# Layer 2's column sums: running sums on GpSimd in place of 25 products with ones each

## The chip, the core and the metric

The kernel runs on one core of a Trainium2 chip. The metric is the device time of one execution in microseconds (us). Before the change it is 3435.26 us, the median of six runs between 3418.8 and 3440.62.

Short names for the engines: PE is TensorE, the matrix engine, whose weight loads are listed as PEld; DVE is VectorE, ACT is ScalarE, POOL is GpSimd, SP is SyncE, which here only issues DMAs. PE writes its products to PSUM, which POOL doesn't read in this kernel.

## The reference

A graph network of four layers on 3125 nodes with 256 features and 100000 edges: a graph convolution, an attention layer, a gated layer and a convolution with a decoder. After each the result is added to `x` and normalized along the features. The change lies in the last step of the attention layer and the first step of the gated one (layer 2), cut here to what matters:

```python
x = _layernorm(x + attention(x, ...), axis=-1)      # layer 1
# layer 2
mean = jnp.mean(feat, axis=0)                       # over the 3125 nodes, for each feature
var = jnp.var(feat, axis=0)
h = (feat - mean) * jax.lax.rsqrt(var + EPS) * gamma + beta
feat_in, feat_out = h @ W_in + b_in, h @ W_out + b_out
a_in = segment_sum(feat_in[src] * iw[:, None], dst)
a_out = segment_sum(feat_out[dst] * ow[:, None], src)
...
```

So layer 2 needs two sums over all nodes for each of the 256 features: of `x`, and of the squares of `x` less its mean.

## The kernel before

The nodes are laid out in 25 blocks (`NBK`) of 128 rows: `x[:, b, :]` is block b, 128 partitions by 256 float32. Block 0 holds few nodes (`FEW_ROWS`, 53), the others are full. A layer's sum over edges is done as a product with a dense slab: for block b, `weighted_slab` builds 25 tiles of 128 x 128 edge weights, and `apply_f32` multiplies them with the features of all 25 blocks, adding up in the PSUM tile `acc` (L783, 25 products of 128 x 257 for a block).

A slab is built in two halves of 13 and 12 tiles. For each half DVE makes the one-hot tiles `os` and `od` (L729) by comparing keys with a row of column numbers, and three products `wo` of `od` with the three bfloat16 parts of the weights (L909); both inputs of all of these lie in SBUF. PE multiplies `wo` with `os` into PSUM tiles `slab` of four tiles each (L755, three buffers), and ACT copies these to SBUF as `slab_f` (L756). `wo` has four buffers, so DVE can't run far ahead of PE. The weights of the next block are split by four short DVE instructions (L899 to L903).

**Attention** is a loop over the 25 blocks, in the pool `layer1`: build the slab, multiply with `H`, then `den` and its reciprocal on DVE (L972, L973), Relu on ACT (`tmp`, L975), add to `x` on DVE (L976), and `norm(b)`: statistics on DVE (L696 to L698), a square root on ACT (L702), reciprocal and the scaling of `x[:, b, :]` on DVE (L703, L704). From L704 on, block b of `x` is final for layer 2's sums. In block 0 `bounds()` takes some extremes for a flag.

**Layer 2's first pass**, in the pools `layer2` and `layer2a`, is again a loop over the 25 blocks: `aggregate` builds the slab and multiplies it with `x`, ACT copies the result (`sums`, L1090), SP writes it to `a_in`, and then `stage(b)` does a share of the side work:

- stage 0 forms the sum of `x` over the nodes: 25 products with a 128 x 128 matrix of ones (`ones_f`; for block 0 `few`, which has ones only in the rows that hold nodes), all into one PSUM tile `mm` (L1027). DVE scales it to `mean` (L1028).
- each stage takes two blocks: POOL subtracts `mean` (L1033, into `away`, two buffers), ACT squares it in place (L1034). The next stage multiplies each of the two with ones into the PSUM tile `var` (named `look` in the profile, L1030).
- stages 14 and 15 copy the keys into another order on POOL (`keys_t`, `keyd_t`, L1038). Stage 16 loads weights and multiplies them together (L1050, PSUM tile `mm`; the pool of `mm` has a single buffer). Stages 17 to 19 make `scl`, `cr`, `cols` and biases from `var`.

The second pass uses the turned keys and these factors, and ends each block with gates and a normalization; layer 3 follows.

The order of the work in attention and layer 2 isn't written out by hand: a planner walks through the program with costs of its own and gives each engine, whenever it is free, the earliest instruction of the program that is ready by those costs. The result is a fixed order for each engine and queue. On the chip each engine then keeps that order and waits by semaphores. So an instruction can run long before its place in the program (keys_t's copy of stage 14 runs ahead of stage 0's subtract), and one that is late on the chip holds up whatever the planner put behind it on its engine. `tc.keep_in_program_order(o)` ties an instruction behind the one before it in the program on the same engine.

Of the kernel before, what the change touches and what calls it, by code (L numbers as in the profile page):

```python
# [8 lines left out]
F32 = mybir.dt.float32  # L9
# [3 lines left out]
OP = mybir.AluOpType  # L13
# [5 lines left out]
P = 128  # L19
# [18 lines left out]
NBK = 25  # L38
# [14 lines left out]
KD = ND // P  # L53
# [46 lines left out]
def dense_path(ctx: ExitStack, tc: tile.TileContext, a: dict, out: bass.AP, flag: bass.AP):  # L100
    nc = tc.nc
    N, D = 3125, ND
# [19 lines left out]
    ones_f = top.tile([P, P], F32, name="ones_f")  # L122
# [517 lines left out]
    psM = ctx.enter_context(tc.tile_pool(name="d_psM", bufs=1, space=PSUM))  # L640
# [15 lines left out]
    x = x1[:, :, 1:D + 1]  # L656
# [268 lines left out]

    with tc.tile_pool(name="layer1", bufs=2) as pool:
        den = pool.tile([P, NBK], F32, name="den", bufs=1)

        def largest(v, n=1):

            vt = psT.tile([P, P], F32, name="tp")
            nc.tensor.transpose(vt[:n, :], v, ident)
            r = pool.tile([n, 1], F32, name=f"largest{n}", bufs=6)
            nc.vector.tensor_reduce(r, vt[:n, :], axis=AX.X, op=OP.max)
            return r


        bmax = pool.tile([P, NBK], F32, name="bmax", bufs=1)
        q_by_target = q.rearrange("p (d t) -> p d t", d=NBK)
        nc.vector.tensor_reduce(bmax, q_by_target, axis=AX.X, op=OP.max)  # L940
        r = largest(bmax, NBK)
        c = psT.tile([P, NBK], F32, name="tp")
        nc.tensor.matmul(c, r.to_broadcast([NBK, P]), ident[:NBK, :NBK], start=True, stop=True)
        nc.vector.tensor_tensor(q_by_target, q_by_target, c[:, :, None].to_broadcast([P, NBK, TS]), op=OP.subtract)
        nc.scalar.activation(q, q, AF.Exp)


        nc.vector.tensor_reduce(ends[:, 2:3], s1, axis=AX.X, op=OP.max)
        nc.vector.tensor_reduce(ends[:, 3:4], s1, axis=AX.X, op=OP.min)
        e4 = pool.tile([P, 4], F32, name="e4", bufs=1)  # L950

        def bounds():
            for i in range(4):
                nc.vector.tensor_scalar(e4[:, i:i + 1], ends[:, i:i + 1], 1.0 if i % 2 == 0 else -1.0, None, op0=OP.mult)
            m4 = [largest(e4[:, i:i + 1]) for i in range(4)]
            zs = []
            for i, sg in ((0, 1.0), (1, -1.0)):
                z = pool.tile([1, 1], F32, name=f"z{i}", bufs=1)
                nc.vector.tensor_tensor(z, m4[i], m4[i + 2], op=OP.add)
                nc.vector.tensor_scalar(z, z, sg, None, op0=OP.mult)  # L960
                nc.vector.scalar_tensor_tensor(z, z, 0.01, z, op0=OP.mult, op1=OP.max)
                zs.append(z)
            nc.vector.tensor_sub(zs[0], zs[0], zs[1])
            nc.vector.tensor_scalar(flag[:, 1:2], zs[0], SPREAD, None, op0=OP.is_ge)

        for b in range(NBK):
            w3 = wk.tile([P, 3, TS, 2], BF, name="w3")
            weights_split(w3, wk, q[:, b * TS:(b + 1) * TS], TS, 2)
            slab = weighted_slab(pool, b, keys, keyd, w3)
            p = apply_f32(slab, H, D + 1)  # L970

            nc.vector.tensor_scalar(den[:, b:b + 1], p[:, D:], 1e-37, None, op0=OP.max)  # L972
            nc.vector.reciprocal(den[:, b:b + 1], den[:, b:b + 1])  # L973
            y = wk.tile([P, D], F32, name="tmp")
            nc.scalar.activation(y, p[:, :D], AF.Relu, scale=den[:, b:b + 1])  # L975
            nc.vector.tensor_add(x[:, b, :], x[:, b, :], y)  # L976
            norm(b)
            if b == 0:
                bounds()

# [6 lines left out]
    with tc.tile_pool(name="layer2", bufs=1) as pool:  # L989
# [27 lines left out]

        with tc.tile_pool(name="layer2a", bufs=1) as pa:
            mean, var = pa.tile([P, D], F32, name="mean"), psL.tile([P, D], F32, name="look")
            squares = {}  # L1020

            def stage(b):

                if b == 0:
                    p = psM.tile([P, 512], F32, name="mm")
                    for i in range(NBK):
                        nc.tensor.matmul(p[:, :D], ones_f if i else few, x[:, i, :], start=(i == 0), stop=(i == NBK - 1))  # L1027
                    nc.vector.tensor_scalar(mean, p[:, :D], 1.0 / N, None, op0=OP.mult)  # L1028
                for i in sorted(squares):
                    nc.tensor.matmul(var, ones_f if i else few, squares.pop(i), start=(i == 0), stop=(i == NBK - 1))  # L1030
                for i in range(2 * b, min(2 * b + 2, NBK)):
                    y = pa.tile([P, D], F32, name="away", bufs=2)
                    nc.gpsimd.tensor_tensor(y, x[:, i, :], mean, op=OP.subtract)  # L1033
                    nc.scalar.activation(y, y, AF.Square)  # L1034
                    squares[i] = y
                if 14 <= b < 16:
                    to, k = ((keys_t, keys), (keyd_t, keyd))[b - 14]
                    nc.gpsimd.tensor_copy(to.rearrange("p (s d j) two -> p d s (j two)", d=NBK, j=TB),  # L1038
                                          k.rearrange("p (d s j) two -> p d s (j two)", s=NBK, j=TB))
                if b == 16:  # L1040

                    load(W_x2i, a["L2_gnn_W_x2i"])
                    biases = pa.tile([P, 2, KD], F32, name="biases")
                    for i, n in enumerate(("in", "out")):
                        nc.scalar.dma_start(biases[:, i, :], a["L2_gnn_b_" + n].rearrange("(k p) -> p k", p=P))
                        t = load(W_T[i], a[f"W_{n}T"])
                        for k in range(KD):
                            p = psM.tile([P, 512], F32, name="mm")
                            for j in range(KD):
                                nc.tensor.matmul(p, t[:, j, k * P:(k + 1) * P], W_x2i[:, i * KD + j, :],  # L1050
                                                 start=(j == 0), stop=(j == KD - 1))
                            nc.scalar.activation(W_x[i][:, k, :], p, AF.Copy)
                    kept.update(biases=biases)
                if b == 17:
                    gamma = load(part(3072, D), a["L2_gnn_gamma"])
                    beta = load(part(3328, D), a["L2_gnn_beta"])
                    nc.vector.tensor_scalar(scl, var, 1.0 / N, EPS, op0=OP.mult, op1=OP.add)
                    nc.scalar.activation(scl, scl, AF.Sqrt)
                    nc.vector.reciprocal(scl, scl)
                    nc.vector.tensor_tensor(scl, scl, gamma, op=OP.mult)  # L1060
                    nc.vector.tensor_tensor(cr, mean, scl, op=OP.mult)
                    nc.vector.tensor_tensor(cr, beta, cr, op=OP.subtract)
                if b == 18:
                    p = psT.tile([P, 4, P], F32, name="tp")
                    for i, v in enumerate(halves(scl) + halves(cr)):
                        nc.tensor.transpose(p[:, i, :], v, ident)
                    nc.vector.tensor_copy(cols.rearrange("p i k -> p (i k)"), p[:, :, 0])
                if b == 19:
                    for i in range(2):
                        p = psM.tile([P, 512], F32, name="mm")  # L1070
                        for k in range(KD):
                            for j, (l, r) in enumerate(((cols[:, 1, k:k + 1], W_x[i][:, k, :]),
                                                        (kept["biases"][:, i, k:k + 1], W_x2i[:, i * KD + k, :]))):
                                nc.tensor.matmul(p, l.to_broadcast([P, P]), r, start=(k == 0 and j == 0),
                                                 stop=(k == KD - 1 and j == 1))
                        nc.scalar.activation(u[:, i, :], p, AF.Copy)
                    p = psM.tile([P, 512], F32, name="mm")
                    for k in range(KD):
                        nc.tensor.matmul(p, cols[:, 1, k:k + 1].to_broadcast([P, P]), W_h2h[:, k, :],
                                         start=(k == 0), stop=(k == KD - 1))  # L1080
                    nc.vector.tensor_add(bx, p, bx)
                    for w in W_x + [W_h2h]:
                        for k in range(KD):
                            nc.scalar.activation(w[:, k, :], w[:, k, :], AF.Copy, scale=cols[:, 0, k:k + 1])
# [745 lines left out]
```

## Time and profile before

The execution that was profiled took 3435.43 us; its span, from the first to the last instruction, is 3433.5 us. The stretches below are from the start of the span; the columns are the time that each engine was busy in them.

| stretch, us | what | length | PE | DVE | ACT | POOL |
|---|---|---|---|---|---|---|
| 0 to 1206 | sorting the edges | 1206.0 | 411.1 | 760.4 | 268.4 | 764.5 |
| 1206 to 1822 | layer 0, scores | 616.0 | 566.3 | 336.8 | 162.1 | 0.4 |
| 1822 to 2229 | attention | 407.3 | 400.5 | 341.5 | 105.3 | 0.0 |
| 2229 to 2665 | layer 2, first pass | 435.7 | 432.1 | 299.7 | 116.9 | 21.3 |
| 2665 to 3270 | layer 2, second pass | 605.0 | 582.6 | 413.4 | 235.8 | 0.0 |
| 3270 to 3433 | layer 3 | 163.5 | 147.5 | 81.6 | 32.6 | 0.0 |

What the lines of the change took: L1027, 50 instructions on PE (a float32 product is two), in two pieces of 4.41 and 6.50 us; L1030, 50 instructions, spread over 13 blocks, two products in each but the last; L1033, 25 on POOL, 16.5 us in sum; L1034, 25 on ACT of 0.42 us.

How to read the lines that are shown: a chain of waits lists, in order of time, when a piece of work began, how long it lay on the chain, its engine, its tile and its line; it is followed back from the last instruction, so what is on it set the end. A timeline line has the start, the length, engine, line and operation, the tiles written and read, and in brackets how long the engine was idle before and what ended that. `x66` after a line counts instructions. A busy PE is not a PE at its peak, since products are pipelined.

### The profile page before, as it was taken

How to read it: one execution, taken by the hardware profiler on the slowest of the kernel's cores; microseconds unless marked ns; L12 is line 12 of the kernel's file. 1: busy time of each engine (PE TensorE's matmuls, PEld its weight loads, DVE VectorE, ACT ScalarE, POOL GpSimd, SP SyncE). 2: the span in 40 equal slices, each digit the busy share in tenths (PEclk: the TensorE clock that was granted, in tenths of full speed). 3: DMA queues.
4: the chain of work that ended last, by engine and by line, in shares of the span. 5: the costliest groups of instructions: out<-in, count | busy, mean ns of one | idle time of the engine just before them, and what ended most of it. 6: DMA issues, size and time to landing. Idle time of an engine off the chain costs nothing.

```text
span 3433.5 us, 60046 instructions
## 1 busy us (share of the span) xinstructions
PE 2540.2 (74%) x25737; PEld 1960.4 (57%) x25737; DVE 2233.3 (65%) x3824; ACT 921.1 (27%) x1827; POOL 786.2 (23%) x874
## 2 busy tenths in 40 slices
PE   4334332332343179999998999999999999999998
PEld 2112121221221068878877888888888777676754
DVE  8676755655656664535558888867766676776645
ACT  3112121221221244430002222222223334343421
POOL 4666666666666500000000000010000000000000
PEclk6555566666656589999998999999999999999999
DMA  4121112122212041146540000010001110100043
GB/s 132 54 66 51 59 55 63 59 63 63 66 49 64 1 137 71 74 148 224 223 173 1 2 2 2 6 43 15 15 15 15 16 12 9 12 9 11 29 138 121
DMA packets 171989, 203.46 MB, mean 59 GB/s; under 512 B 119719, under 2 KB 144796, under 8 KB 165441
## 3 DMA queue, kind: packets, MB, share of 16 engines
q1 hardware_dynamic: 134698, 188.26, 17.1%
q10 hardware_dynamic: 11927, 9.63, 1.0%
q0 software_dynamic: 25088, 1.66, 0.7%
q8 instruction: 203, 3.33, 0.4%
q14 instruction: 73, 0.60, 0.1%
HBM read 167.60 MB, written 31.86 MB: 58 GB/s over the span
## 4 chain that ended last, share of the span: by engine, by line
PE 49%; DVE 21%; another core or an unknown queue 16%; ACT 8%; issue 3%; DMA 2%; POOL 1%; ACTq 0%; DVEq 0%; POOLq 0%; SPq 0%
PE acc L783 17%; PE acc L775 11%; PE mm L687 6%; PE slab L755 5%; DVE wo L909 3%; PE acc L1156 3%; DVE os L729 3%; DVE eq L465 2%; PE tp L680 2%; DVE rank L469 1%; ACT dT L453 1%; ACT away L452 1%; DVE eam L459 1%; DVE rec L460 1%
## 5 line engine op out<-in xcount | busy, mean ns | idle before, releaser
L498 POOL DMA_INDIRECT table<-rec,row x784 | 754.7, 963 | 332.0 <-issue 222.4
L783 PE MATMUL acc<-x,slab_f 128*128 128x257 f32 x2500 | 592.5, 386 | 0.0
L909 DVE TENSOR_TENSOR wo<-od,w 128x1664 bf16<-128x1664 bf16 (+1 forms) x450 | 434.5, 985 | 134.6 <-PE slab L755 108.4
L783 PEld LDWEIGHTS acc<-x,slab_f 128*128 128x128 f32 x2500 | 455.8, 189 | 71.4 <-issue 5.8
L361 PE MATMUL place<-by_target,op 128*128 128x100 bf16 x392 | 40.9, 281 | 506.5 <-ACT tick L512 348.2
L775 PEld LDWEIGHTS <-wo 128*128 128x128 bf16 x3750 | 363.4, 98 | 47.8 <-issue 3.2
L729 DVE TENSOR_TENSOR os<-iota_b,keys 128x3328 bf16<-128x3328 bf16 (+1 forms) x150 | 273.0, 1820 | 115.2 <-PE slab L755 114.1
L755 PEld LDWEIGHTS <-os 128*128 128x128 bf16 x8750 | 296.7, 98 | 80.5 <-ACT q L821 32.4
L361 PEld LDWEIGHTS <-op 128*128 128x128 bf16 x392 | 33.0, 136 | 518.7 <-issue 385.4
L783 PE MATMUL acc<-features,slab_f 128*128 128x257 f32 x1250 | 296.9, 388 | 0.0
L755 PE MATMUL slab<-wo,os 128*128 128x64 bf16 x7500 | 261.1, 193 | 13.4 <-ACT slab_f L756 8.2
L783 PEld LDWEIGHTS acc<-features,slab_f 128*128 128x128 f32 x1250 | 227.9, 190 | 43.3 <-issue 12.1
L756 ACT ACTIVATE slab_f<-slab 128x512 f32<-128x512 f32 (+1 forms) x350 | 182.5, 548 | 145.9 <-PE slab L755 138.2
L775 PE MATMUL acc<-H,wo 128*128 128x256 bf16 x1875 | 218.9, 273 | 0.0
L775 PE MATMUL acc<-features,wo 128*128 128x256 bf16 x1875 | 212.4, 273 | 0.0
L482 DVE TENSOR_TENSOR sel<-place,by_source 128x400 f32<-128x400 f32 (+1 forms) x52 | 28.4, 547 | 251.6 <-PE place L361 134.3
L512 ACT ACTIVATE tick<-place 1x1 f32<-1x1 f32 x48 | 7.7, 160 | 645.7 <-remote 557.1
L465 DVE TENSOR_SCALAR eq<-gap 128x512 bf16<-128x512 f32 x196 | 123.8, 684 | 80.6 <-remote 46.0
L475 PE MATMUL place<-pre,dT 52*128 52x25 bf16 x784 | 29.9, 175 | 187.2 <-DVE both L365 69.7
L1038 POOL COPY keys_t<-keys 128x2500 bf16<-128x2500 bf16 x1 | 2.5, 2522 | 720.7 <-ACT tmp L975 720.7
L729 DVE TENSOR_TENSOR od<-iota_b,keyd 128x1664 bf16<-128x1664 bf16 (+1 forms) x150 | 147.9, 986 | 0.0
L767 PEld LDWEIGHTS <-wo 128*64 128x64 bf16 x3750 | 112.0, 110 | 47.5 <-issue 47.5
(286 smaller groups left out, 3769.9 us busy)
## 6 DMA issues: line engine op xcount, KB each, us to landing
ea<-in_edge_attr SPq DMA_DIRECT2D x49, 1024.0 KB
wo<-slabs SPq DMA_DIRECT2D x50, 800.0 KB
os<-rows SPq DMA_DIRECT2D x25, 832.0 KB
slabs<-wo SPq DMA_DIRECT2D x25, 800.0 KB
od<-rows SPq DMA_DIRECT2D x25, 768.0 KB
table<-rec,row POOLq DMA_INDIRECT x784
dr<-db_row SPq DMA_DIRECT2D x48, 208.0 KB
rec_b<-table SPq DMA_DIRECT2D x75, 100.0 KB
```

Source lines behind the costliest of these rows:

```text
L361: nc.tensor.matmul(deg, op[:, c:c + 2, :], od[:, c:c + 2, :TS], start=(c == 0), stop=(c == CH - 2), skip_group_check=True)
L465: nc.vector.tensor_scalar(eq[:, 4 * g:4 * g + 4, :], of[k]["gap"][g], 0.0, None, op0=OP.is_equal)
L498: i = nc.gpsimd.indirect_dma_start(out=table, out_offset=bass.IndirectOffsetOnAxis(ap=ready[k][:, c:c + 1], axis=0), in_=rec[:, k * CH + c ...
L687: nc.tensor.matmul(p[:, :m], l, r, start=(i == 0), stop=(i == len(w) - 1))
L729: nc.vector.tensor_tensor(in_pairs(t[:, :n, :]), repeat(iota_b[:, :cols], n), pair(k, cols), op=OP.is_equal)
L755: nc.tensor.matmul(p[:, i - g, own], l, r, start=(m == 0), stop=(m == len(terms) - 1))
L756: nc.scalar.activation(dst[:, g:g + w, :], p[:, :w, :], AF.Copy)
L767: nc.tensor.matmul(p[j * HP:(j + 1) * HP, i - g, :], stat[:, i * TB + j, :], mov[:, i * TB + j, :], start=(m == 0), stop=(m == len(stats) ...
L775: nc.tensor.matmul(p[:, :m], slab[:, s, :], parts[:, s, k, :m], start=(s == 0 and k == 0), stop=(s == NBK - 1 and k == 2))
L783: nc.tensor.matmul(p[:, :m], t[:, s, :], H[:, o + s, :m], start=(o + s == 0), stop=(o + s == NBK - 1))
L909: nc.vector.tensor_tensor(in_pairs(t[:, :n, :]), in_pairs(oh[:, :n, :]), pair(w3[k], HP), op=OP.mult)
L1156: nc.tensor.matmul(acc[b][:, :3 * F0], slab[b][:, s, :], H3[:, s].rearrange("p k m -> p (k m)"), start=(s == 0), stop=(s == NBK - 1))
```

## The change

In attention, a new tile `total` of 128 x 256 float32 in attention's pool takes the sum of the blocks 1 to 24 of `x`: after block 2's normalization POOL adds blocks 1 and 2 into it, and after each later block's it adds that block, 23 additions in all. A PSUM tile `of_all` (from the pool of `mm`) is taken in block 0 and gets two products behind the loop: `few` with block 0, and `ones_f` with `total`. Stage 0 only scales it to `mean`.

In the first pass, the square of block 1 is made in a tile `squares` (also called `total`), and POOL adds the squares of the blocks 2 to 24 to it, 23 additions. `var` gets two products, `few` with block 0's square and `ones_f` with the sum. The subtracts on POOL and the squares on ACT stay. The first product of stage 16 is tied behind PE's work before it in the program.

```diff
     with tc.tile_pool(name="layer1", bufs=2) as pool:
         den = pool.tile([P, NBK], F32, name="den", bufs=1)
+        total = pool.tile([P, D], F32, name="total", bufs=1)
...
             norm(b)
             if b == 0:
                 bounds()
+                of_all = psM.tile([P, 512], F32, name="mm")
+            elif b == 2:
+                nc.gpsimd.tensor_tensor(total, x[:, 1, :], x[:, 2, :], op=OP.add)
+            elif b > 2:
+                nc.gpsimd.tensor_tensor(total, total, x[:, b, :], op=OP.add)
+        for l, r in ((few, x[:, 0, :]), (ones_f, total)):
+            nc.tensor.matmul(of_all[:, :D], l, r, start=(l is few), stop=(l is ones_f))
...
-            squares = {}
+            squares, total = {}, pa.tile([P, D], F32, name="squares")
...
                 if b == 0:
-                    p = psM.tile([P, 512], F32, name="mm")
-                    for i in range(NBK):
-                        nc.tensor.matmul(p[:, :D], ones_f if i else few, x[:, i, :], start=(i == 0), stop=(i == NBK - 1))
-                    nc.vector.tensor_scalar(mean, p[:, :D], 1.0 / N, None, op0=OP.mult)
+                    nc.vector.tensor_scalar(mean, of_all[:, :D], 1.0 / N, None, op0=OP.mult)
                 for i in sorted(squares):
-                    nc.tensor.matmul(var, ones_f if i else few, squares.pop(i), start=(i == 0), stop=(i == NBK - 1))
+                    y = squares.pop(i)
+                    if i == 0:
+                        nc.tensor.matmul(var, few, y, start=True, stop=False)
+                    else:
+                        nc.gpsimd.tensor_tensor(total, total, y, op=OP.add)
+                    if i == NBK - 1:
+                        nc.tensor.matmul(var, ones_f, total, start=False, stop=True)
                 for i in range(2 * b, min(2 * b + 2, NBK)):
-                    y = pa.tile([P, D], F32, name="away", bufs=2)
+                    y = total if i == 1 else pa.tile([P, D], F32, name="away", bufs=2)
                     nc.gpsimd.tensor_tensor(y, x[:, i, :], mean, op=OP.subtract)
                     nc.scalar.activation(y, y, AF.Square)
-                    squares[i] = y
+                    if i != 1:
+                        squares[i] = y
...
-                                nc.tensor.matmul(p, t[:, j, k * P:(k + 1) * P], W_x2i[:, i * KD + j, :],
-                                                 start=(j == 0), stop=(j == KD - 1))
+                                o = nc.tensor.matmul(p, t[:, j, k * P:(k + 1) * P], W_x2i[:, i * KD + j, :],
+                                                     start=(j == 0), stop=(j == KD - 1))
+                                if i == k == j == 0:
+                                    tc.keep_in_program_order(o)
```

## The prediction

> **What bounds the kernel now.** I read the page's slices first, then busy time by stage, then the chain that ended last, cut to one block of attention, to the seam into layer 2, and to the first pass. The slices show where the change lies: attention runs from 1822 to 2229 us, layer 2's first pass from there to about 2665, and in both PE is busy nine tenths or more at nearly full granted clock, while POOL is empty but for a spot at the seam.
>
> ```profile
> span 3433.5 us, 60046 instructions
> PE   4334332332343179999998999999999999999998
> POOL 4666666666666500000000000010000000000000
> PEclk6555566666656589999998999999999999999999
> ```
>
> Busy time by stage puts numbers on it (columns: stretch, its length, then PE, PEld, DVE, ACT and POOL busy, PE clock, DMA). DVE has 66 us to spare in attention and 136 in the first pass; PE has 7 and 4.
>
> ```profile
> 1822.00:2229.30 407.30, 400.53 (x4996) 346.99 (x4996) 341.47 (x573) 105.26 (x224) 0.00 (x0) 0.99 0.01 2
> 2229.30:2665.00 435.70, 432.10 (x5139) 372.78 (x5138) 299.65 (x393) 116.94 (x239) 21.32 (x27) 1.00 0.08 21
> ```
>
> A busy PE is not yet the bound. The chain through one attention block (start, us, what) shows that each block passes once through DVE and ACT: after the last product of `acc` come den, Relu, the normalization up to L704, then two `wo` products on DVE, and only then the next slab on PE. A block takes 16.26 us (1878.78 to 1895.03 and so on).
>
> ```profile
> 2004.55 0.41 DVE x L704
> 2004.96 1.74 DVE wo L909 x2
> 2006.71 0.04 issue
> 2006.75 2.08 PE slab L755 x66
> ```
>
> So the two `wo` that follow L704 have no slack: PE starts 0.04 us after them. The rest of DVE's work in the block has some, since DVE waits 1.46 us for PE before den.
>
> The chain at the seam and in the first pass shows the products to be removed, and a second path: POOL's subtract and ACT's square stand ahead of the slab copies in ACT's order, so they too end a wait of PE.
>
> ```profile
> 2231.52 4.41 PE mm L1027 x20
> ...
> 2249.42 6.50 PE mm L1027 x30
> ...
> 2256.46 1.33 POOL away L1033 x2
> 2257.78 0.02 issue
> 2257.81 0.42 ACT away L1034
> 2258.22 0.98 ACT slab_f L756 x2
> 2259.20 0.04 issue
> 2259.24 0.19 PE slab L755
> ```
>
> **The change part by part.** The profiled execution took 3435.43 us (span 3433.5 and 1.93 around it), 0.17 over the median of 3435.26, so the sum needs no correction for it.
>
> *Mean products, from 25 to 2.* Each is two instructions on PE: 50 in 4.41 + 6.50 = 10.91 us, 0.218 each. The second piece, 6.50, goes whole. The first piece partly fills a wait: without it PE would be at its next slab at 2231.5, but the first slab copy on ACT starts only at 2232.77 and takes 0.55, so 2233.3 is the earliest instead of 2235.9, a gain of at most 2.6. It can be less. The last add needs block 24 after L704, which ended at 2233.15; POOL's 0.66 and PE's two instructions (0.44) lead to 2234.3, and if the copies wait for that (the new tile lies in attention's pool, and keys_t's copy waited for den's last reader in that pool) PE goes on about 2234.8. I take 1.5 for this piece and 0.44 for the product with `few`: 6.50 + 1.5 - 0.44 = **7.6** gained. Ends: 6.50 - 0.87 = 5.6 with the first piece worth nothing, and 6.50 + 2.6 - 0.44 + 0.9 (PE's waits at 2258 to 2259 gone as well) = 9.6.
>
> *Square products, from 25 to 2.* Twelve blocks, 2263.49 to 2464.96, take 201.47 us, 16.79 each; blocks without squares take 15.68 (2481.63, 2497.31, 2512.99). Twelve at 15.68 are 188.16, so 13.31 goes, 0.44 for the single product in the thirteenth comes on top and 0.87 stays: **12.9** gained. Of the 1.11 per block only 0.87 is PE's own work; the rest is the wait behind ACT. If that stays, it is 10.0; if the wait at 2258 also goes with it, 13.8 (counted in one term only).
>
> *Adds in attention, 23 on POOL.* POOL is empty there, and a subtract of this shape took 1.32 us for two, 0.66 each; in itself this costs nothing. The question is whether it holds DVE up. It is released when L704 of its block ends, about 0.08 later (as the first subtract was behind `mean`), hence while the first of the two `wo` without slack is running. Three rows bear on it:
>
> ```profile
> 2230.44 0.43 DVE L976 TENSOR_TENSOR x<-x,tmp 128x256 f32<-128x256 f32 x1 [0.63 <-ACT tmp L975]
> 2232.21 0.94 DVE L704 TENSOR_SCALAR x<-x,stats,rstd 128x256 f32<-128x256 f32 x1
> 2230.47 2.52 POOL L1038 COPY keys_t<-keys 128x2500 bf16<-128x2500 bf16 x1 [720.70 <-ACT tmp L975]
> 2232.95 2.32 POOL L1038 COPY keyd_t<-keyd 128x2500 bf16<-128x2500 bf16 x1
> ```
>
> L704, 0.41 in the other blocks, took 0.94 here, and ended 0.16 after the keys copy, with POOL's next copy already behind it. L976 began just ahead of that copy and kept its usual 0.43, and the copy took 0.2 longer than its twin. So who comes later waits for the other's instruction, and gets its turn before the other's next one. By this the add waits for the first `wo`, goes next, and the second `wo` waits for the add. The rows are of a one-input DVE instruction, so it is bounded: nothing (POOL gets in where DVE rests), or 22 blocks with a single subtract's 0.72, 15.8. I take the row that is nearest, L704's 0.53 extra and the add's 0.66, as 0.6: 22 x 0.6 = **13.2** lost. The 23rd add has no pair behind it. A gain is excluded: no row lets DVE go sooner.
>
> [...]
>
> *Adds and squares in the first pass.* POOL has 25 subtracts and 23 adds, 48 x 0.66 = 31.7 us instead of 16.5. Before, the next subtract waited for the products on PE, which set one pair per block (15.5 us of idle each), when DVE was at rest. Now the buffers come free by POOL's own add, and only block 0's square still waits for PE. The planner issues what is ready: keys_t's copy belongs to stage 14 and ran ahead of stage 0's subtract; the second pass's first `tmp` (L1108) ran at 2489.6. So the squares will run in one go, in ACT's order between slab copies that were planned without any hold by DVE. DVE works 10.6 of 15.68 us a block, so rests 5.1. POOL's 31.7 against this rest is 31.7 - 2 x 5.1 = 21.5 left over if the squares are packed into two blocks (31.7 us is the length of two), 8.8 in four and a half, nothing above six. What is left over stands in DVE's way, or holds a square and the slab copies behind it. Ends nothing and 21.5; with packing likely but the chain through ACT stretching it, I take **8.8** lost.
>
> *The rest.* The pin on L1050 keeps its products behind PE's earlier work; they ran at 2522, after stage 15's blocks anyway: nothing, and if they moved up they would only fill time. `mean` is ready up to 20 us sooner; what is late next is PE itself at 15.68 a block. Variance ends sooner, while scl, cr and cols have nothing waiting until 2561.
>
> Sum: -7.6 - 12.9 + 13.2 + 8.8 = +1.5, 3436.9, rounded to **3437 us**.
>
> **The rivals.** *POOL hinders nobody:* adds slip into DVE's rests (1.46 before den, 5.1 in the first pass). L976 speaks for it, L704 against. Then -20.5 and some 2 for squares that come late: 3435.4 - 18.5 = 3417, faster.
>
> *ACT's order turns against it* (slower): squares packed into two blocks, POOL late, ACT waits at a square and the slab copies queued behind it, with PE behind them. For it: exactly this wait is in the chain at 2256 to 2259, and ACT waited 7.4 us there. Against: DVE falls idle as soon as PE does, which lets POOL catch up. Price 21.5, with 15.8 in attention: -20.5 + 15.8 + 21.5 = +16.8, 3452. It decides from 17.6 us in the first pass, where the sum passes +10.3.
>
> *The seam eats the gain:* the keys copies (4.84 us) get ahead of the last add, or hold DVE's `wo` there. Then the mean's first piece turns from 1.5 gained into some 3 lost: 3437 + 4.5 = 3441.
>
> **How the numbers follow.** A difference under 0.3%, 10.3 us, can't be told from no change here; the six times themselves span 22. Forecast 0.36, seam 0.06, POOL hinders nobody 0.25, ACT's order 0.33. That gives faster 0.25, same 0.42, slower 0.33. The forecast's own range is 3426 to 3446; both sign cases lie within 3415 (all the gains at 20.5, no cost) and 3457 (the slow case with 5 more in the seam), which should leave out no more than 2 in 10.
>
> **What would show it.** Right: L1027's line and `look` with 4 instructions each; POOL with 71 TENSOR_TENSOR; an attention block near 16.9 with the second `wo` after L704 at 1.5 instead of 0.95; first-pass blocks at 15.68 once the squares are through, with longer ones before, in the first four or five. Wrong for attention: blocks still at 16.26. Wrong for the first pass: squares spread one pair to a block, or blocks at 15.68 from the start (faster), or ACT waiting over 10 us for `away` in sum (slower). What would make it wrong most is the hold between POOL and DVE, which 23 blocks and 48 instructions multiply.

## The result and the profile after

The changed kernel takes 3456.73 us (median of 20 runs, 3440.49 to 3470.69), the kernel before, run beside it, 3432.82 (46 runs). The ratio is 1.0069 with a 95% interval of 1.0058 to 1.0080: 23.9 us slower.

The slices of the page after:

```profile
span 3449.0 us, 59940 instructions
...
PE   4333334333333099999979999969999999999998
...
POOL 4766666666666400000000000150000000000000
PEclk6555555656665599999989999989999999999999
```

POOL's digits show the squares packed into two slices behind attention, where before there was one spot of 1. In the second of them PE falls to 6 and its clock to 8. POOL's adds in attention are too short for a digit.

Busy time by stage of the changed kernel (stretch, length, then PE, PEld, DVE, ACT and POOL busy, PE clock, DMA), cut at attention's end and where the third block of the first pass (block 2) begins its products `acc`:

```profile
1822.00:2230.84 408.84, 391.51 (x4841) 338.69 (x4840) 344.59 (x563) 101.56 (x218) 27.69 (x22) 1.00 0.01 2
2230.84:2307.78 76.94, 47.36 (x565) 38.39 (x565) 44.74 (x45) 20.85 (x49) 52.27 (x51) 0.82 0.13 43
2307.78:2672.00 364.22, 363.19 (x4444) 311.73 (x4444) 260.51 (x338) 98.30 (x190) 0.00 (x0) 1.00 0.07 16
```

The second row holds the result. Before, this stretch (2229.42 to 2280.30) was 50.88 us long with PE busy for 49.83 of them; now PE stands for 29.6. In the third row PE is the bound again, at 15.68 us a block.

The three differences, each from two rows of the trace. From attention's first `acc` to its end: 409.4 us, before 398.7 (+10.7). From there to block 2's `acc`: 76.9, before 50.9 (+26.1). From there to the last block's `acc`: 364.1, before 376.3 (-12.2). Sum +24.6, where the medians differ by 23.9; all that follows is within 0.2 us of what it was. The two spans differ by only 15.5 us (3449.0 and 3433.5), because in this execution of the changed kernel attention's first `acc` came 9.3 us earlier; no edit touches what lies ahead of it, and executions of one kernel span some 30 us, so that part is taken as chance and left out of the sum.

One attention block of the changed kernel, first by the chain of waits, then the two engines of the same place by the timeline:

```profile
1999.12 0.41 DVE x L704
1999.54 2.19 DVE wo L909 x2
2001.72 0.04 issue
2001.77 2.08 PE slab L755 x66
```

```profile
1999.45 2.27 DVE L909 TENSOR_TENSOR wo<-od,w 128x1536 bf16<-128x1536 bf16 x2
1999.68 1.22 POOL L985 TENSOR_TENSOR total<-total,x 128x256 f32<-128x256 f32 x1 [15.49 <-DVE x L704]
```

The two `wo` behind L704 lie on the chain for 2.19 us, 1.74 before. The add, 0.64 long where it is alone (at 2234.17), shows 1.22: it waits through the first `wo`, and the second waits for it. Blocks take 16.70 and 16.79 us in turn instead of 16.26, as the pair takes 2.27 and 2.35 instead of 1.82.

In the first pass the chain of waits of the changed kernel goes through POOL and ACT, one square at a time, and ACT's timeline shows what stood behind the squares:

```profile
2261.94 0.73 POOL squares L1039
2262.74 0.65 POOL away L1044
2263.41 0.43 ACT away L1045
...
2263.90 0.73 POOL squares L1039
...
2264.70 0.73 POOL away L1044
2265.45 0.42 ACT away L1045
```

```profile
2269.46 0.42 ACT L1045 ACTIVATE away<-away 128x256 f32<-128x256 f32 x1 [1.63 <-POOL away L1044]
2271.42 0.42 ACT L1045 ACTIVATE away<-away 128x256 f32<-128x256 f32 x1 [1.55 <-POOL away L1044]
2271.74 0.37 ACT L1104 ACTIVATE sums<-acc 128x257 f32<-128x257 f32 x1
2273.47 0.42 ACT L1045 ACTIVATE away<-away 128x256 f32<-128x256 f32 x1 [1.35 <-POOL away L1044]
2273.79 1.06 ACT L756 ACTIVATE slab_f<-slab 128x512 f32<-128x512 f32 x2
```

In ACT's order nine squares stand in a row ahead of block 0's `sums` and the next slab copies (L756), and four ahead of block 1's `sums`. A square costs some 2.0 us: subtract, square, add, in a ring, because one of the two buffers of `away` is held by block 0's square until its product on PE at 2294.18. The waits of this stretch (waiting engine, for whom, us in total, times, longest) carry the rest of the reading:

```profile
ACT away L1045 <- POOL away L1044: 44.8, 24, 4.3
DVE wo L909 <- PE slab L755: 29.3, 4, 18.2
...
PE slab L755 <- ACT slab_f L756: 22.6, 4, 16.9
```

ACT waits for POOL, PE for ACT, and DVE for PE: three engines rest behind the ring. Of PE's 29.6 us the longest wait, 16.9, lies behind the nine squares.

### The profile page after: what moved, and what is told of

The parts are those of the page before. It is cut to its first block, busy times and chain, and to the rows that moved or that the text cites. A ratio compares the mean times of both kernels' runs of the same rounds, so it can differ in the third digit from the quotient of the medians.

```text
span 3449.0 us, 59940 instructions
## 1 busy us (share of the span) xinstructions
PE 2545.2 (74%) x25645; PEld 1950.8 (57%) x25645; DVE 2258.2 (65%) x3824; ACT 923.8 (27%) x1827; POOL 844.9 (24%) x920
## 3 DMA queue, kind: packets, MB, share of 16 engines
q1 hardware_dynamic: 134698, 188.26, 16.9%
## 4 chain that ended last, share of the span: by engine, by line
PE 48%; DVE 21%; another core or an unknown queue 17%; ACT 8%; issue 2%; POOL 2%; DMA 2%; ACTq 0%; DVEq 0%; SPq 0%; POOLq 0%
PE acc L783 16%; PE acc L775 11%; PE mm L687 6%; PE slab L755 5%; DVE wo L909 4%; PE acc L1170 3%; DVE os L729 3%; PE tp L680 2%; ACT dT L453 2%; ACT away L452 2%; DVE eq L465 1%; DVE rank L469 1%; DVE eam L459 1%; ACT L1126 1%
## 5 line engine op out<-in xcount | busy, mean ns | idle before, releaser
L783 PE MATMUL acc<-x,slab_f 128*128 128x257 f32 x2500 | 600.5, 388 | 5.5 <-ACT slab_f L756 5.5
L909 DVE TENSOR_TENSOR wo<-od,w 128x1664 bf16<-128x1664 bf16 (+1 forms) x450 | 450.6, 1020 | 142.1 <-PE slab L755 115.8
L756 ACT ACTIVATE slab_f<-slab 128x512 f32<-128x512 f32 (+1 forms) x350 | 185.0, 548 | 159.8 <-PE slab L755 150.4
L420 PEld LDWEIGHTS <-by_target 128*52 128x52 bf16 x784 | 90.4, 137 | 78.0 <-issue 54.1
```

The lines of the kernel that those rows point to most:

```text
L420: nc.tensor.matmul(cnt[:, c + 1:, :], it["by_target"][:, c], it["by_source"][:, c:c + 1, :].to_broadcast([P, CH - c, KB]), start=False, st ...
L756: nc.scalar.activation(dst[:, g:g + w, :], p[:, :w, :], AF.Copy)
L783: nc.tensor.matmul(p[:, :m], t[:, s, :], H[:, o + s, :m], start=(o + s == 0), stop=(o + s == NBK - 1))
L909: nc.vector.tensor_tensor(in_pairs(t[:, :n, :]), in_pairs(oh[:, :n, :]), pair(w3[k], HP), op=OP.mult)
```

## The experiments

Each experiment has the kernel before run beside it: e1 to e4 one set (3428.99 us), e5b to e8 another (3427.78), e9 to e11 a third (3271.10), e12 a fourth (3271.78). In the last two sets the kernel before took some 157 us less, and in the traces the stretch ahead of attention, which no edit touches, is some 160 us shorter; so only ratios and stretches of the trace are compared across sets.

The table gives, from the traces, attention's length (first `acc` to its end), then when block 0 and block 2 of the first pass and the first block of the second pass start `acc`, counted from attention's end, and the ratio. Before and the change stand first. With a dash block 0's `acc` starts and stops again behind squares, or is kept back by products that moved ahead of it (e9). e4, e6 and e7 stand in the text.

| kernel | attention | block 0 | block 2 | second pass | ratio, interval |
|---|---|---|---|---|---|
| before | 398.7 | 10.8 | 50.9 | 443.0 | 1 |
| the change | 409.4 | - | 76.9 | 456.9 | 1.0069 [1.0058, 1.0080] |
| e1 | 409.5 | 13.6 | 46.1 | 438.3 | 1.0003 [0.9988, 1.0019] |
| e2 | 398.7 | 10.8 | 79.6 | 459.6 | 1.0047 [1.0030, 1.0065] |
| e3 | 409.5 | 12.5 | 45.0 | 427.6 | 0.9979 [0.9965, 0.9993] |
| e5b | 399.7 | 12.5 | 45.0 | 427.6 | 0.9958 [0.9943, 0.9973] |
| e8 | 409.5 | - | 78.0 | 458.1 | 1.0072 [1.0047, 1.0097] |
| e9 | 409.5 | - | 76.3 | 454.1 | 1.0063 [1.0047, 1.0078] |
| e10 | 399.7 | 13.2 | 45.7 | 428.3 | 0.9955 [0.9942, 0.9969] |
| e11 | 399.7 | 9.6 | 42.1 | 429.4 | 0.9983 [0.9974, 0.9992] |
| e12 | 399.7 | 17.0 | 49.7 | 432.2 | 0.9969 [0.9957, 0.9981] |

**e1, attention's half alone.** The sum of `x` as changed, the squares with 25 products as before:

```diff
-                    y = squares.pop(i)
-                    if i == 0:
-                        nc.tensor.matmul(var, few, y, start=True, stop=False)
-                    else:
-                        nc.gpsimd.tensor_tensor(total, total, y, op=OP.add)
...
+                    nc.tensor.matmul(var, ones_f if i else few, squares.pop(i), start=(i == 0), stop=(i == NBK - 1))
```

> The attention half alone: running sum of x on POOL and two products for the mean, while the squares keep their 25 products with ones. Theory A (POOL's add holds the second of DVE's two wo behind L704): attention blocks near 16.75 us as with the whole change, 0.49 over before's 16.26, 10.8 us in sum; the mean's products give back some 7 (the second piece of 6.5 whole, the first next to nothing, because PE restarted as late after attention with the change as before it), first-pass blocks back at 16.8. So 3 to 5 us slower than before. Rival (the seam between the layers costs, not attention): blocks at 16.26 and the time up by 10 or more through PE's wait at the seam. Rival (attention costs nothing by itself): faster than before by 7.

3432.86 us. Attention is 10.8 us longer, block 2 comes 4.8 earlier: +6.0 by the trace, +3.9 by the medians, and the interval holds both and nothing at all.

**e2, the squares' half alone.** The mean with 25 products as before, no adds in attention:

```diff
-            elif b == 2:
-                nc.gpsimd.tensor_tensor(total, x[:, 1, :], x[:, 2, :], op=OP.add)
-            elif b > 2:
-                nc.gpsimd.tensor_tensor(total, total, x[:, b, :], op=OP.add)
...
+                    for i in range(NBK):
+                        nc.tensor.matmul(p[:, :D], ones_f if i else few, x[:, i, :], start=(i == 0), stop=(i == NBK - 1))
```

> The first-pass half alone: squares summed on POOL, the mean from 25 products as before, attention as before. Theory A (the planner packs the squares into ACT's order ahead of slab copies in the first blocks, and PE waits for these): the changed kernel lost 13.9 us from attention's end to the last block of the pass against before, with 6.5 of the mean's products gained in it, so this one should be some 20 us slower than before, with two or three long blocks at the start and 15.68 afterwards. Rival (the loss lies in the seam made by attention's running sum): the pass is 12 us shorter than before. Rival (POOL's work delays DVE in every block): all the blocks with squares are longer by about 1 us.

3445.83 us, 16.8 more than before, and 16.6 by the trace. Block 0 starts as before, block 2 is 28.8 us late. So the hole in the first pass belongs to the squares alone, whatever the mean is made of.

**e3, the squares held at their stage.** The whole change, with each square tied behind ACT's earlier work:

```diff
-                    nc.scalar.activation(y, y, AF.Square)
+                    tc.keep_in_program_order(nc.scalar.activation(y, y, AF.Square))
```

> The whole change, but each stage's squares on ACT are tied behind ACT's work before them in the program, so two squares a block stand after the block's sums copy; POOL does the same 48 instructions. Orders on PE and DVE are the same as with the change. Theory A (packing in ACT's order): the third block's product starts some 42 us after attention's end instead of 77, all blocks near 15.7, so some 34 us faster than the changed kernel and 10 faster than before, with attention still at 16.75. Rival (DVE and POOL holding each other is what costs in the pass, not the order on ACT): POOL's work is the same, so blocks with squares stay 1 us or more above 15.68, and only some 10 to 20 us are won.

3421.91 us. The orders of PE, DVE and SP are the changed kernel's; ACT's differs, and with it the order in which POOL takes its subtracts and additions. By the ratios some 31 us go (1.0069 to 0.9979). The stretch from attention's end to block 2 by stage, then ACT's timeline in it:

```profile
2239.96:2284.97 45.01, 41.43 (x565) 35.76 (x565) 34.71 (x43) 12.70 (x28) 14.92 (x11) 0.96 0.22 73
```

```profile
2277.35 0.39 ACT L1104 ACTIVATE sums<-acc 128x257 f32<-128x257 f32 x1 [8.59 <-PE acc L783]
2277.63 0.41 ACT L1045 ACTIVATE away<-away 128x256 f32<-128x256 f32 x1
2278.56 0.42 ACT L1045 ACTIVATE away<-away 128x256 f32<-128x256 f32 x1 [0.53 <-POOL away L1044]
2278.89 1.76 ACT L756 ACTIVATE slab_f<-slab 128x512 f32<-128x512 f32 x4
```

PE has the same 565 instructions here and 45.0 us instead of 76.9. Two squares now follow each `sums`, and the slab copies come right behind. While squares last a block takes 15.95 instead of 15.68: beside POOL's subtracts a pair of `wo` takes 2.35 instead of 1.83 and the `os` behind it 2.32 instead of 1.88 (2328.32 to 2332.92), and 0.27 of this reaches the block.

**e4, the adds moved, to a place that wasn't one.** As e1, with block b-2's add tied behind the weight split of block b:

```diff
+            if b > 3:
+                add_up(b - 2, split_done)
```

> The attention half alone, as the first run here, but POOL adds block b-2 only behind the last DVE instruction of the weights split of block b, which ends just before DVE rests for 1.46 us waiting for PE; the last two adds stand behind the loop. Theory A (the place of the add decides): attention blocks at 16.26, 10.8 us less than the first run, 6 to 8 faster than before. Rival (an add costs some 0.5 us wherever it stands): blocks stay at 16.7 and the time equals the first run's.

3429.77 us, 1.0004 [0.9989, 1.0019], a miss. The split of block b runs before block b-2 is normalized, so the add was released by L704 as before and blocks stayed at 16.75. It says nothing on the place.

**e5b, the adds in DVE's rest, and the squares held.** As e3, with block b-3's add behind the split of block b, the last three behind the loop:

```diff
+            split_done = weights_split(w3, wk, q[:, b * TS:(b + 1) * TS], TS, 2)
+            if b > 4:
+                add_up(b - 3, split_done)
...
-                    nc.scalar.activation(y, y, AF.Square)
+                    tc.keep_in_program_order(nc.scalar.activation(y, y, AF.Square))
```

> The whole change with the squares on ACT tied to their stage, and with POOL's add of block b-3 placed behind the weights split of block b (one block further back than in the fourth run, where block b-2 was not yet normalized and so the add stayed behind L704). Theory A (the add costs only where it meets the two wo behind L704): attention blocks at 16.26 but for the last two or three, some 9 to 10 us less than with the squares tied alone, so 3412, 0.5% faster than before. Rival (an add costs some 0.5 us wherever it stands): the same time as with the squares tied alone, 3422.

3411.92 us, 0.9958 [0.9943, 0.9973]: faster than both kernels, by 15.9 us against the one before. The timeline of one block:

```profile
2008.26 0.64 POOL L968 TENSOR_TENSOR total<-total,x 128x256 f32<-128x256 f32 x1 [15.53 <-DVE w L903]
2012.30 0.41 DVE L704 TENSOR_SCALAR x<-x,stats,rstd 128x256 f32<-128x256 f32 x1
2012.62 1.82 DVE L909 TENSOR_TENSOR wo<-od,w 128x1536 bf16<-128x1536 bf16 x2
```

The add runs 4 us ahead of L704, at its own 0.64, and the pair is back at 1.82. Blocks take 16.26, but for the two at the end, whose adds are behind L704 again.

**e6 and e7, what of POOL's instruction holds DVE.** At the add's place, e6 writes 128 x 1024 zeros and reads nothing, e7 copies the block instead of adding it:

```diff
+            elif b >= 2:
+                i = nc.gpsimd.memset(wide, 0.0)
+                tc.add_manual_dep(i.ins, normed.ins.name, DATA, reason="it runs where the addition ran")
```

> The attention half alone, but at the place of each add POOL fills a tile of 128x1024 with zeros, which reads nothing from SBUF and lasts about as long; the sum over the blocks 1 to 24 is left out, so the mean and all behind it are wrong. Theory A (it is POOL's reading that meets the second input of wo): attention blocks at 16.26. Rival (any work of POOL at this place, or its semaphores, hold DVE): blocks at 16.7.

```diff
+            elif b >= 2:
+                nc.gpsimd.tensor_copy(total, x[:, b, :])
```

> The attention half alone, but POOL copies block b instead of adding it: one input read from SBUF instead of two; the sum over the blocks 1 to 24 is left out, so the mean and all behind it are wrong. Theory A (reading by POOL holds the second wo for as long as POOL's instruction takes): blocks longer than 16.26 by the copy's own length, which I put between 0.3 and 0.5 us. Rival (only POOL's two-input form holds DVE): 16.26.

Each ran once (3427.16 and 3429.59 us), so they are read by the trace alone. The `wo` pair and POOL's instruction by the timelines, of e6 and then of e7:

```profile
2002.52 1.82 DVE L909 TENSOR_TENSOR wo<-od,w 128x1536 bf16<-128x1536 bf16 x2
2002.72 0.95 POOL L984 MEMSET wide<- 128x1024 f32 x1 [15.31 <-DVE x L704]
```

```profile
2002.52 2.02 DVE L909 TENSOR_TENSOR wo<-od,w 128x1536 bf16<-128x1536 bf16 x2
2002.73 1.00 POOL L983 COPY total<-x 128x256 f32<-128x256 f32 x1 [15.47 <-DVE x L704]
```

Nothing is lost beside the write (blocks of 16.26), 0.20 beside the copy (16.46), 0.45 or 0.53 beside the add (2.27 and 2.35). So it is POOL's reading that holds the second `wo`, and for longer with two inputs than with one. Whether `wo`'s second input matters, as e6's text has it, no run shows. Neither text on e7 came: the copy takes 0.40 where it is alone (at 2233.21), and DVE lost half of that.

**e8, a second buffer for the chain.** Block 0's square goes into `scl`'s tile, so that both buffers of `away` turn:

```diff
-                    y = total if i == 1 else pa.tile([P, D], F32, name="away", bufs=2)
+                    y = (scl, total)[i] if i < 2 else pa.tile([P, D], F32, name="away", bufs=2)
```

> The whole change, with block 0's square in a tile of its own (the tile of scl, idle until then), so that both buffers of away are there for the chain, instead of one held until PE's product with block 0's square 64 us later. The order on ACT is still packed. Theory A (the chain of subtract, square and add, one at a time, sets how long ACT holds the slab copies): the chain falls from some 2.0 us for each square to about 1.4, POOL's two instructions, and the whole is 8 to 15 us faster than the change, 3443 to 3448. Rival (DVE's and POOL's holds set the length, not the buffer): less than 4 us.

3451.16 us, 1.0072 [1.0047, 1.0097]: no gain. The chain did speed up, as ACT's timeline of e8 shows, two squares in 2.75 us:

```profile
2254.49 0.42 ACT L1045 ACTIVATE away<-away 128x256 f32<-128x256 f32 x1 [1.76 <-POOL away L1044]
2255.08 0.42 ACT L1045 ACTIVATE away<-away 128x256 f32<-128x256 f32 x1 [0.17 <-POOL away L1044]
2257.24 0.42 ACT L1045 ACTIVATE away<-away 128x256 f32<-128x256 f32 x1 [1.74 <-POOL away L1044]
```

It was through after 49.4 us instead of 62.7, but the planner now has fourteen squares in a row ahead of block 0's `sums` instead of nine; PE's longest wait for ACT was 16.0 us again, and block 2 came after 78.0. What stands ahead of the copies sets the loss, and a faster ring was filled with more: the theory had the pace right and its price wrong, and the rival's number came (no gain) for a reason that it didn't name.

**e9, without the tie on L1050's products.**

```diff
-                                if i == k == j == 0:
-                                    tc.keep_in_program_order(o)
```

> The whole change, with the first product of L1050 not tied to its place. Theory: those products run long after the two blocks in which the squares are packed, so the pin costs and gains nothing: ratio 1.0069 as with the change, within 0.0015, block 2's acc some 77 us after attention's end. Rival: without it the products move up into PE's waits of the first pass's first two blocks, which were over 25 us together, and up to 7 us are gained (ratio about 1.005).

1.0063 [1.0047, 1.0078], not told apart from the change. The trace is between the two texts: two of the eight products, with their four instructions, did move up into the first block (2083.10, after waiting 2.7 us for a load), and the second pass starts 2.8 us earlier than in the change. If the tie costs anything, it is less than 3 us.

**e10 and e11, the seam.** e10 is e5b with the running sum in a tile outside attention's pool; e11 is e10 with the two copies of the keys held at stages 14 and 15:

```diff
-        total = pool.tile([P, D], F32, name="total", bufs=1)
+        total = wk.tile([P, D], F32, name="tmp2", bufs=1)
```

> As e5b, with the running sum, of x and then of the squares, in a tile that lives outside the attention's pool, so that layer 2's first loads and slab copies need not wait for the sum's last reader on PE. In e5b block 0's acc starts 12.5 us after attention's end, 10.8 in the kernel before. Theory: the wait behind the sum's last reader goes, 1 to 4 us shorter there, 3408 to 3411 where e5b gives 3412. Rival: PE waits at the seam for the last block's own chain and for the copies of the keys on POOL anyway, so it is 12.5 again and the time that of e5b within 1 us.

```diff
-                    nc.gpsimd.tensor_copy(to.rearrange("p (s d j) two -> p d s (j two)", d=NBK, j=TB),
-                                          k.rearrange("p (d s j) two -> p d s (j two)", s=NBK, j=TB))
+                    tc.keep_in_program_order(
+                        nc.gpsimd.tensor_copy(to.rearrange("p (s d j) two -> p d s (j two)", d=NBK, j=TB),
+                                              k.rearrange("p (d s j) two -> p d s (j two)", s=NBK, j=TB)))
```

> As e10_kept_total, with POOL's two copies of the keys, which run at the seam (2.3 to 3.1 us each), held back to stages 14 and 15, where the program has them. Theory: at the seam nothing of POOL but the last adds is in the way of DVE and of the first subtract, so layer 2's first block starts 1 to 3 us earlier, 3406 to 3409. Rival: the copies then stand in DVE's way in stages 14 and 15 for the same 2 to 4 us, and the time is that of e10_kept_total within 1 us.

e10: the ratio of e5b, as its rival had it, with block 0 after 13.2 us. The copies, free of the pool too, now got ahead of the last add, which began at 2071.73 behind both. e11: block 0 after 9.6 us, 3.6 earlier; but the copies, now right behind POOL's last addition, stood beside a `wo` pair ahead of block 13, which took 5.24 instead of e10's 1.83:

```profile
2284.29 2.26 POOL L1056 COPY keys_t<-keys 128x2500 bf16<-128x2500 bf16 x1
2285.06 5.24 DVE L909 TENSOR_TENSOR wo<-od,w 128x1536 bf16<-128x1536 bf16 x2 [3.62 <-PE slab L755]
2286.50 2.99 POOL L1056 COPY keyd_t<-keyd 128x2500 bf16<-128x2500 bf16 x1
```

That block took 20.31 instead of 15.68, and the 3.6 were given back. In time e11 is slower than e10 by 9.6 us; by the traces only 1.2 of it lies behind attention's start, and 6.1 of the profiled execution's 7.3 lie in the sorting ahead of it, in the same instructions. What made these longer is left open.

**e12, PE kept busy at the seam.** As e5b, with idle products:

```diff
+        spare = psL.tile([P, D], F32, name="look")
...
+            for _ in range(2 if i else 0):
+                nc.tensor.matmul(spare, ones_f, x[:, NBK - 1, :], start=True, stop=True)
...
+        for _ in range(4):
+            nc.tensor.matmul(spare, ones_f, total, start=True, stop=True)
```

> As e5b, with six idle products on PE at the seam, two of block 24 with ones ahead of the sum's product and four of the sum behind it, 0.44 us each, into a tile that nobody reads; they fill the two waits of 1.5 and 1.7 us in which PE stands there. Nothing that the output needs is left out. Theory: the removed mean products had kept PE busy at the seam and so its clock open; in e1, e5b and the changed kernel PE stands 3.2 of some 6.4 us there, the granted clock of the next stretch is 0.59 to 0.76 instead of 1.00, and the same small products take up to twice as long. With PE busy the clock stays at 1.00 and block 0's acc starts 9.5 to 11 us after attention's end, where e5b has 12.5: 1.5 to 3 us gained. Rival: POOL's copies of the keys, which stand in the way of DVE's wo at the seam, set that pace; then it stays at 12.5, or gets later by the idle products, up to 1 us. In the time itself (3412 in e5b, ratio 0.9958) 2 us is 0.0006, which the interval won't tell; the trace will.

Two rows of PE's timeline behind the seam, of e5b and then of e12, which had PE busy until 2072.73, and then two of e12's stretches (columns as above):

```profile
2229.43 1.21 PE L783 MATMUL acc<-x,slab_f 128*128 128x257 f32 x2
```

```profile
2075.21 0.68 PE L783 MATMUL acc<-x,slab_f 128*128 128x257 f32 x2
```

```profile
2072.73:2076.41 3.68, 1.45 (x13) 1.07 (x13) 1.60 (x1) 1.75 (x4) 3.68 (x4) 1.00 0.80 252
2076.42:2083.19 6.77, 5.84 (x74) 5.07 (x74) 6.71 (x6) 1.19 (x2) 2.26 (x1) 0.50 0.00 2
```

Right behind the idle products the same product went through at the pace of a full clock. But PE then stood again, 1.77 us for ACT and 0.66 for DVE, and the granted clock was 0.50 all the way to block 0's `acc`: the products put the fall off and did not keep the clock, so the theory isn't borne out. Block 0 came after 17.0 us, and the second pass starts 4.6 later than in e5b; the ratios (0.9969 and 0.9958) can't be told apart. Three things add up here, and no run parts them. ACT's issue of a load (L666), which has the slab copies behind it, went out at 2072.89, 0.16 after the last idle product, so the first copy started only at 2073.84, 1.9 us later than in e5b counted from attention's end. Then both copies of the keys stood beside the first `wo` pair, which took 4.69 us (2.63 in e5b); this is the rival's cause. And the slow clock lasted for 6.8 us.

## Where the prediction was right and wrong, step by step

Its sum was +1.5 us, measured was +23.9; 3456.73 lies just inside the upper end of the range, 3457. The case that came was the rival "ACT's order turns against it" (3452), not the forecast, and that the rival's total comes so near is partly luck: attention cost 5 us less than it says and the first pass 10 more.

*Mean products, 7.6 gained: 4.8 by e1.* The second piece brought more than the 6.50 that was counted: block 0 to block 1 takes 15.7 us in e1 and 23.3 before, 7.6, so PE's wait at 2258 to 2259, which the prediction had only in its upper end, went too. The first, taken for 1.5 gained, lost 2.8, as the rival "the seam eats the gain" had it, though not by the copies that it names. The step that failed is that PE's next slab at an earlier time would be a gain. It was hardly earlier (6.4 us after attention's end, before 6.5): the sum's product ended at 2236.34, the issue of L666's load on ACT went out at 2236.42, and the first slab copy behind it started at 2237.36, so the wait for the new tile that the prediction named came, and was longer. In e10, with the tile outside attention's pool, that copy starts 3.4 us after attention's end, in e1 5.7. And it ran slower. Busy time by stage from attention's end to PE's restart and on to block 0's `acc`, before and then in e1:

```profile
2229.42:2235.93 6.51, 6.51 (x98) 5.87 (x95) 2.61 (x8) 2.25 (x5) 4.79 (x2) 1.00 0.86 276
2235.93:2240.22 4.29, 4.29 (x87) 3.80 (x84) 4.13 (x4) 1.47 (x3) 0.00 (x0) 1.00 0.70 210
```

```profile
2231.62:2238.01 6.39, 3.22 (x76) 2.64 (x76) 2.52 (x9) 1.32 (x4) 2.17 (x2) 0.93 0.82 282
2238.01:2245.25 7.24, 7.24 (x87) 5.94 (x87) 6.83 (x4) 3.13 (x7) 7.24 (x4) 0.59 0.44 133
```

The same 87 instructions on PE take 7.24 us at a granted clock of 0.59, 4.29 at 1.00. PE waits for nothing in these 7.24 us, and the pair of `wo`, 2.53 long beside POOL's subtracts, ended 1.6 us before PE took it up, so here it is the clock that shows; at a full clock (2.95 us less) DVE would, by my estimate from these numbers, have been next to hold PE up, as in e12. Before, the removed products had filled PE's wait, and the clock stayed at 1.00. e11, whose PE stood for only 1.7 us at this place, kept 1.00. In e1 PE stood in two pieces, of 1.51 and 1.67 us with a product of 0.70 between them; how long it has to stand for the clock to fall, the runs don't show. I read that PE's products there filled a wait, and counted them as free to remove.

*Square products, 12.9 gained: right.* Blocks without squares take 15.68 from block 2 on, as said; the 12.2 in the third difference above lack only what fell into the hole.

*Adds in attention, 13.2 lost: 10.7.* The mechanism was the predicted one: the add waits for the first `wo`, the second for the add, 22 times, and e5b's adds in DVE's rest lose nothing. In calling its rows those of a one-input instruction the prediction misread one: L976 reads two, `x` and `tmp`. The size was 0.49 a block, not 0.6: the add takes 0.64, but DVE lost less than that, and more than the 0.20 beside e7's copy.

*First pass, 8.8 lost, at most 21.5: some 30 to 32.* This is the term that failed. With the mean's and the adds' terms as measured (-4.8, +10.7) and the squares' as predicted (-12.9) it must be 31.6 for the traces' sum of 24.6; in e2, which has the squares alone, it is 29.5 in the same way (16.6 + 12.9); and block 2 in e3, with the squares tied to their stage, comes 31.9 earlier than in the change. The prediction had the packing, and ACT waiting with slab copies behind it, but two steps of its price were wrong. It took POOL's 31.7 us of work, less what fits into DVE's rests, for the price; the chain was a ring through ACT with one free buffer, 62.7 us. (The rest was misread as well: 5.1 us a block, where DVE is busy for 11.69 of the 15.68 us from 2497.31 to 2512.99, so rests 4.0; by its own sum the worst would have been 23.7.) And it took for granted that, when DVE falls idle, POOL catches up; with DVE idle the ring still took some 2.0 us a square, and PE, DVE and ACT all stood while the squares ahead of the copies went by one by one. The length alone isn't the price either: e8's ring, at 1.4 us a square, was through in 49.4 us and saved nothing, since the planner put more squares in a row.

*The rest.* The tie on L1050's products counted as nothing: within 3 us by e9. Most signs named to look for came: four instructions on PE for each sum, 71 additions and subtractions on POOL, and the rival's sign, ACT waiting far more than 10 us for `away` (44.8). The long blocks were the first two, as the rival had it, not the first four or five.

## What to carry to other kernels

Work moved to an idle engine is priced by what queues behind it: look up what stands behind every step of the new chain in the order of each engine that it passes, and tie side work to its place in the program when it is ready early. Count a removed piece of work on PE as a gain only if PE doesn't stand in its place; PE that has stood can come back at a lower clock (0.59 in e1). And an instruction on POOL that reads SBUF belongs where DVE rests, not behind the event that makes its data ready: here the same additions cost 10.7 us in one place and 1.0 in the other.

## What the runs showed of the hardware

- A reading POOL instruction that was released during one of two back-to-back `wo` of DVE (two inputs from SBUF) got in between them, each time (22 times in the change, where the adds show 1.14 to 1.31 us instead of 0.64). DVE lost 0.45 and 0.53 us in turn (0.49 on average) to an addition of 128 x 256 float32 and 0.20 to a copy, nothing to a write of 128 x 1024 (16.26 us a block in e6). In these runs the hold is shorter than POOL's whole instruction, 0.64 for an addition and 0.40 for a copy where they are alone.
- PE idle for half of a stretch of 6.4 us had a granted clock of 0.59 in the next 7.2 (e1), after the same in the change 0.76 (2237.23 to 2244.40); there, 10.7 us with 5.9 of them busy (2290.00 to 2300.65) were followed by 0.62 in the 7.1 us before block 2. In e12 3.7 us with 1.45 of them busy were followed by 0.50 in the next 6.8. Idle for 1.7 us at the seam left it at 1.00 (e11).
